# Composed weights permuted on TensorE, part of a projection and a third of the first loads moved to GpSimd, in an attention and mixture-of-experts kernel

## The chip, the cores and the metric

The kernel runs on one core of a Trainium2 chip. The metric is the time of one execution on the device in microseconds, the median of three runs. A core has five engines that run at their own pace and wait for each other by semaphores: TensorE (PE in the profile, PEld for its weight loads), VectorE (DVE), ScalarE (ACT), GpSimd (POOL) and SyncE (SP). SP does no arithmetic here; it issues DMA transfers. POOL and ACT can issue transfers too. Each engine works through its own list of instructions strictly in order.

## The reference, cut to what matters

The input is x of 4 elements x 1024 tokens x 256 channels. The kernel computes causal attention with 16 heads of 16 numbers, adds x and normalizes, then a layer of 8 experts of which each token uses 2, adds and normalizes again. The part that the change touches is the projection of x to queries and keys:

```python
q_lat = (x @ Wq_down).reshape(b, t, H, L)          # the same for k and v
q_c = jnp.einsum('bthl,ld->bhtd', q_lat, Wq_up_c)  # content half of a head
q_e = jnp.einsum('bthl,ld->bhtd', q_lat, Wq_up_e)  # half that is rotated
q = jnp.concatenate([q_c, _apply_rope(q_e, cos, sin)], axis=-1)
scores = jnp.einsum('bhqd,bhkd->bhqk', q, k) * scale
att = jax.nn.softmax(jnp.where(causal, scores, -jnp.inf), axis=-1)
y = jnp.einsum('bhqk,bhkd->bhqd', att, v)
```

## The kernel before, in words

**Composed weights.** The kernel multiplies each down matrix with its up matrix once, at its start, so that a projection is one product of x with a 256 x 256 matrix. The loop over n (0 for queries, 1 for keys, 2 for values) does this: `weffT{n}` (L206, eight products of ups and down), a copy to SBUF as `wT{n}` (L211, DVE), and four transposes by TensorE to `weff{n}` (L215). Every operand of a projection is kept as a high part (rounded to the fp32r type of TensorE, made by ACT, L190) and a low part (the rest, made by DVE or POOL, L191); the helper `split` makes both. For n = 0 and 1 the columns of `weff` must be brought from the order "pair of heads, dimension, head in the pair" to the order "dimension, head"; the kernel does this while splitting, in six pieces for each n, through a strided view.

**Projection.** `project(b, half, ...)` handles 512 tokens of element b. It splits x (`xT_h`, `xT_l`), computes four chunks of 128 rows of queries and keys (`qk_ps`: chunk 2 is the content of q, 3 the content of k, 0 and 1 the two members of the pairs to rotate for q and k), each as six products (`mm3`, L197 to L199), rotates chunks 0 and 1 (products with the table `rope`, L283 and L285, and their sum `t`, L286), and cuts each result into three bf16 parts (`store`: `lv`, with the remainder `r` between; L261, L263, L264, L265). The parts go to DRAM (`parts`, L268). Then come the values (`v_ps`, `va`). The name `lean` says which engine makes the low parts, the sums and the last bf16 part: DVE for element 0, POOL for the others. Most of the tiles have a single buffer: a second `r` or `t` can only be written when the first has been read.

**Loads of a stack.** `load_stack(unit, halves)` reads the bf16 parts of a group of four heads back from DRAM in six slots of 16 rows (c = 0 to 5) for queries (`qs`) and keys (`ks`): twelve transfers, all issued by SP (L338). The first unit (element 0, group 0) is loaded in two calls, one for each half of the tokens, because attention on the first half needs only that. Until the first half's twelve transfers have landed, there is nothing for attention to do.

**Attention.** For each unit `row_max` computes the scores (`s`, L353 and for the diagonal L370), their maxima on DVE (L374, L383), and puts the negated maxima as two extra rows into `qs` (L399). `attend` computes the scores again, transposed (`sT`, L456), the exponentials on ACT (`pT`, L462), masks the diagonal block on POOL (L474), and multiplies with the values (`y`, L437). After the attention come the experts.

**Order.** The kernel is written with a tile framework that simulates its timeline when the program is built and lets that decide the order of each engine's list. An edit in one place therefore moves instructions elsewhere. Once built, the order of every list is fixed.

Of the kernel before, what the change touches and what calls it, by code (L numbers as in the profile page):

```python
# [9 lines left out]
F32 = mybir.dt.float32  # L10
# [25 lines left out]
P = 128  # L36
# [7 lines left out]
def kernel(  # L44
# [16 lines left out]
    nc = tc.nc  # L61
    B, T, C = x_in.shape
    DH = ups_in.shape[2] // 2
    DHE = DH // 2
    H = C // DH
    E, _, FF = wg_in.shape
    NB = T // P
    CC = C // P
# [34 lines left out]
    proj = pctx.enter_context(tc.tile_pool(name="proj", bufs=1))  # L103
# [12 lines left out]
    def any_tile(name):  # L116

        turn[0] += 1
        return (mx_tile, bg_tile, mx_tile, st_tile, bg_tile, mx_tile, st_tile)[turn[0] % 7](name)
# [19 lines left out]
    def load_x(b, half):  # L139
        t = proj.tile([P, CC, QC], F32, tag="x_half", name=f"xh{b}_{half}")  # L140
        nc.sync.dma_start(
            out=t, in_=x_t[b, :, half * QC : (half + 1) * QC].rearrange("(c p) t -> p c t", p=P)
        )
        x_half[b, half] = t
# [10 lines left out]

    ident = const.tile([P, P], F32, name="ident")
    make_identity(nc, ident)
    ident_b = const.tile([P, P], BF16, name="ident_b")
    nc.vector.tensor_copy(ident_b, ident)

# [18 lines left out]
    wqk_h = proj.tile([P, CC, 4 * P], F32R, name="wqk_h")  # L179
    wqk_l = proj.tile([P, CC, 4 * P], F32R, name="wqk_l")  # L180
    wv_h = proj.tile([P, CC, C], F32R, name="wv_h")
    wv_l = proj.tile([P, CC, C], F32R, name="wv_l")
# [5 lines left out]
    def split(hi, lo, src, sub=None):  # L188

        nc.scalar.copy(hi, src)  # L190
        (sub or nc.vector).tensor_tensor(lo, src, hi.bitcast(F32), ALU.subtract)  # L191

    def mm3(ps, terms):

        n = len(terms)
        for i, (sh, sl, mh, ml) in enumerate(terms):
            nc.tensor.matmul(ps, lhsT=sh, rhs=mh, start=(i == 0), stop=False)  # L197
            nc.tensor.matmul(ps, lhsT=sh, rhs=ml, start=False, stop=False)  # L198
            nc.tensor.matmul(ps, lhsT=sl, rhs=mh, start=False, stop=(i == n - 1))  # L199


    for n in range(3):
        acc = any_tile(f"weffT{n}")
        for i in range(H // 2):
            at = i % 4 * 2 * DH
            nc.tensor.matmul(  # L206
                acc[at : at + 2 * DH, i // 4 * C : (i // 4 + 1) * C], lhsT=ups[:, n], rhs=down[n][:, i],
                start=True, stop=True,
            )
        wT = proj.tile([P, QC], F32, tag="r", name=f"wT{n}", bufs=R_BUFS)  # L210
        nc.vector.tensor_copy(wT, acc)  # L211
        acc = any_tile(f"weff{n}")
        for c in range(CC):
            for i in range(2):
                nc.tensor.transpose(  # L215
                    acc[:, (c * 2 + i) * P : (c * 2 + i + 1) * P], wT[:, i * C + c * P : i * C + (c + 1) * P], ident
                )
        if n == 2:
            split(wv_h, wv_l, acc.rearrange("p (c m) -> p c m", c=CC))
            continue  # L220
        for c in range(CC):

            src = acc[:, c * C : (c + 1) * C].rearrange("p (a d i) -> p d a i", d=DH, i=2)
            for d0, d1, at in ((0, DHE, (2 + n) * P), (DHE, DHE + 4, n * 4 * H), (DHE + 4, DH, P + n * 4 * H)):
                hi, lo = (
                    w[:, c, at : at + (d1 - d0) * H].rearrange("p (d a i) -> p d a i", a=H // 2, i=2)
                    for w in (wqk_h, wqk_l)
                )
                split(hi, lo, src[:, d0:d1])


    WAIT = -1.0
# [3 lines left out]
    def project(b, half, tile_):  # L236
        if half == 0:
            parts[b] = dram.tile([2, NQC, 3, DH, H, QC], BF16, name=f"parts{b}", tag="parts", bufs=2)
        pd = parts[b]
        n = f"{b}_{half}"  # L240
        xh = x_half.pop((b, half))
        cols = slice(half * QC, (half + 1) * QC)
        lean = nc.gpsimd if b else nc.vector
        hi = proj.tile([P, CC, QC], F32R, tag="xT_h", name=f"xT_h{n}")
        lo = proj.tile([P, CC, QC], F32R, tag="xT_l", name=f"xT_l{n}")
        for c in range(CC):
            split(hi[:, c], lo[:, c], xh[:, c], lean)
        yield 0.2
        if half + 1 < NQC or b + 1 < B:
            load_x(b + (half + 1) // NQC, (half + 1) % NQC)  # L250

        def chunk(k):
            ps = tile_(f"qk_ps{n}_{k}")
            cut = slice(k * P, (k + 1) * P)
            mm3(ps, [(wqk_h[:, c, cut], wqk_l[:, c, cut], hi[:, c], lo[:, c]) for c in range(CC)])
            return ps

        def store(k, src, sub, rows):

            lv = proj.tile([P, 3, QC], BF16, tag=f"lv{k}", name=f"lv{n}_{k}")  # L260
            nc.scalar.copy(lv[:, 0], src)  # L261
            r = proj.tile([P, QC], F32, tag="r", name=f"r{n}_{k}", bufs=R_BUFS)
            sub.tensor_tensor(r, src, lv[:, 0], ALU.subtract)  # L263
            nc.scalar.copy(lv[:, 1], r)  # L264
            lean.tensor_tensor(lv[:, 2], r, lv[:, 1], ALU.subtract)  # L265
            at = 0
            for qk, row, m in rows:
                (nc.gpsimd if b else nc.sync).dma_start(  # L268
                    out=pd[qk, half, :, row : row + m].rearrange("k d h t -> (d h) k t"),
                    in_=lv[at : at + m * H],  # L270
                )
                at += m * H

        for qk in range(2):
            store(2 + qk, chunk(2 + qk), nc.vector, [(qk, 0, DHE)])
            yield 1.3
        pair = []
        for o in range(2):
            pair.append(chunk(o))
            yield 1.3  # L280
        for o in range(2):
            t1 = proj.tile([P, QC], F32, tag="t1", name=f"t1_{n}_{o}", bufs=R_BUFS)
            nc.vector.tensor_tensor(t1, pair[o], rope[:, 2 * o, cols], ALU.mult)  # L283
            t2 = proj.tile([P, QC], F32, tag="t2", name=f"t2_{n}_{o}", bufs=R_BUFS)
            nc.vector.tensor_tensor(t2, pair[1 - o], rope[:, 2 * o + 1, cols], ALU.mult)  # L285
            lean.tensor_tensor(t1, t1, t2, ALU.add)  # L286
            store(o, t1, lean, [(qk, DHE + o * DHE // 2, DHE // 2) for qk in range(2)])
            yield 0.2
        while b >= 2 and not attended.get(b - 2):
            yield WAIT  # L290
        dst = va[b % 2][:, half * BPQ : (half + 1) * BPQ, : H * VW]
        for i in range(0, BPQ, 2):
            ps = tile_(f"v_ps{n}_{i}")
            for j in range(2):
                tok = slice((i + j) * P, (i + j + 1) * P)
                mm3(
                    ps[:, j * C : (j + 1) * C],
                    [(hi[:, c, tok], lo[:, c, tok], wv_h[:, c], wv_l[:, c]) for c in range(CC)],
                )
            for j in range(2):  # L300
                nc.scalar.copy(
                    dst[:, i + j].rearrange("p (h d) -> p h d", d=VW)[:, :, :DH],
                    ps[:, j * C : (j + 1) * C].rearrange("p (h d) -> p h d", d=DH),
                )
            yield 1.3
# [3 lines left out]
    units = [(b, (g,), tuple(range(NQC))) for b in range(B - 1) for g in range(NG)]  # L309
# [13 lines left out]
    queued = [None]  # L323

    def load_stack(unit, halves=None):
        b, gs, qcs = unit
        i = units.index(unit) % NST
        for gi, g in enumerate(gs):
            heads = slice(g * HG, (g + 1) * HG)


            for c, qk_parts in enumerate(((0, 0), (0, 1), (0, 2), (1, 0), (1, 1), (2, 0))):
                for qk, tiles in enumerate((qs, ks)):
                    wanted = halves or (range(qcs[-1] + 1) if qk else qcs)
                    f0, f1 = wanted[0], wanted[-1] + 1
                    s0 = gi if qcs == (0,) else f0
                    rows = tiles[i][:NROW].rearrange("(d c) f h t -> d c f (h t)", c=6)
                    queued[0] = nc.sync.dma_start(  # L338
                        out=rows[:, c, s0 : s0 + f1 - f0],
                        in_=parts[b][qk, f0:f1, qk_parts[qk], :, heads].rearrange("f d h t -> d f (h t)"),  # L340
                    )
# [771 lines left out]
    for i, unit in enumerate(units):  # L1113
        b, gs, qcs = unit
# [22 lines left out]
        for n, over in enumerate(attend(unit)):  # L1137
# [20 lines left out]
            at = n - HG * BPQ * (len(qcs) - 1)  # L1158
# [191 lines left out]
```

## Time and profile before

| what | value |
|---|---|
| median of 3 runs | 1103.49 us (1098.18 to 1103.93) |
| the profiled execution | 1052.3 us, span 1050.5 us |
| mean granted TensorE clock in it | 0.976 |
| busy share of the span: PE, PEld | 92%, 57% |
| DVE, ACT, POOL | 70%, 60%, 46% |
| instructions in the span | 18000 |

The span runs from the first to the last instruction of the one execution that the profiler recorded. That execution was 51 us shorter than the median of the runs. Times in the trace are microseconds from the start of the span. A row of the timeline gives start, duration, engine, line, what is written and what is read, and in brackets how long the engine had been idle and what ended the wait.

### The profile page before, as it was taken

Reading aid. Unit: us, or ns where it says so; the run is one execution under the profiler, and the core shown is the slowest. Engines: PE = TensorE matmul, PEld = TensorE weight load, DVE = VectorE, ACT = ScalarE, POOL = GpSimd, SP = SyncE. Lnnn points to the kernel's source line nnn. Section 1 sums busy time; section 2 is a strip of 40 time slices with the busy share of each in tenths; the row PEclk is TensorE's granted clock in tenths of the full one; section 3 lists DMA queues with packets and bytes.
Section 4 is the critical chain, followed back from the end, with each engine's and each line's share of the span. In section 5 each row is a group of like instructions: output and inputs, shape, how many; then the busy total and the mean of one; then the engine's idle time right before and its main releaser. Section 6 shows DMA issues by size and latency. Waiting matters only on the chain.

```text
span 1050.5 us, 18000 instructions
## 1 busy us (share of the span) xinstructions
PE 964.0 (92%) x6392; PEld 600.2 (57%) x6392; DVE 735.5 (70%) x1630; ACT 625.1 (60%) x1314; POOL 480.9 (46%) x551
## 2 busy tenths in 40 slices
PE   6689999999999999999899999999999999999960
PEld 4555433355544545554344444378888888888960
DVE  4777887888988887688547898285685546555636
ACT  3445766665666666566665676665654546565633
POOL 7176521120451813354323323754477875654535
PEclk9899999999999999999999999999999999999995
DMA  6574421221421403324222420176473765655638
GB/s 257 167 212 133 119 70 45 82 82 41 132 70 57 127 6 118 111 66 122 66 66 78 116 66 2 23 241 164 104 169 90 144 143 124 175 116 137 139 55 320
DMA packets 71362, 119.66 MB, mean 114 GB/s; under 512 B 16416, under 2 KB 43040, under 8 KB 70880
## 3 DMA queue, kind: packets, MB, share of 16 engines
q1 hardware_dynamic: 48544, 81.76, 24.7%
q0 software_dynamic: 20672, 36.41, 16.0%
q8 instruction: 52, 0.85, 0.3%
q10 hardware_dynamic: 2048, 0.27, 0.2%
q14 instruction: 46, 0.38, 0.1%
HBM read 82.52 MB, written 35.60 MB: 112 GB/s over the span
## 4 chain that ended last, share of the span: by engine, by line
PE 73%; DVE 8%; DMA 6%; ACT 5%; SPq 3%; issue 3%; POOL 2%; ACTq 0%; DVEq 0%; POOLq 0%
PE y L437 13%; PE s L353 11%; PE sT L456 11%; PE gp L198 3%; SPq L338 3%; PE gp L199 3%; PE gp L197 3%; PE eo L197 3%; PE eo L198 3%; PE eo L199 3%; PE po L623 2%; ACT pT L462 2%; PE s L370 2%; PE lp L199 2%; PE lp L198 2%
## 5 line engine op out<-in xcount | busy, mean ns | idle before, releaser
L462 ACT ACTIVATE pT<-sT 128x512 f32<-128x512 f32 (+1 forms) x608 | 326.6, 576 | 160.9 <-PE sT L456 132.4
L374 DVE TENSOR_REDUCE mx<-s 128x1 f32<-128x384 f32 (+3 forms) x352 | 215.8, 632 | 41.6 <-PE s L370 40.2
L353 PE MATMUL s<-ks,qs 96*128 96x512 bf16 (+3 forms) x768 | 211.7, 330 | 15.1 <-DMA ks<-parts 7.7
L456 PE MATMUL sT<-qs,ks 98*128 98x512 bf16 (+3 forms) x768 | 212.9, 329 | 8.8 <-ACT pT L462 6.7
L474 POOL TENSOR_SCALAR_AFFINE_SELECT pT<-pT 128x512 f32<-128x512 f32 x120 | 75.7, 637 | 270.7 <-ACT pT L462 263.8
L383 DVE TENSOR_REDUCE mx<-s 128x1 f32<-128x512 f32 x256 | 171.2, 681 | 30.9 <-PE s L353 29.8
L437 PE MATMUL y<-pT,va 128*32 128x512 f32 (+3 forms) x1536 | 171.3, 501 | 1.0 <-POOL pT L474 0.6
L1028 POOL DMA_INDIRECT results<-eo,ents x64 | 105.3, 1646 | 79.1 <-ACT eo L1027 65.1
L353 PEld LDWEIGHTS <-qs 96*128 96x128 bf16 x768 | 70.8, 99 | 110.8 <-issue 83.2
L456 PEld LDWEIGHTS <-ks 98*128 98x128 bf16 x768 | 68.9, 98 | 95.0 <-issue 61.9
L370 PE MATMUL s<-mask,ident_b 128*128 128x128 bf16 (+2 forms) x352 | 86.6, 247 | 0.0
L1011 DVE TENSOR_TENSOR relu<-relu,lp 128x512 f32<-128x512 f32 x64 | 43.7, 683 | 60.2 <-ACT relu L1010 37.3
L191 DVE TENSOR_TENSOR wl<-w,wh 128x512 fp32r<-128x512 f32 x108 | 69.6, 684 | 22.3 <-ACT wh L190 20.7
L197 PE MATMUL eo<-wh,hh 128*128 128x256 f32 x280 | 80.9, 291 | 2.7 <-ACT eo L1027 2.2
L198 PE MATMUL eo<-wl,hh 128*128 128x256 f32 x280 | 78.7, 283 | 0.0
L954 POOL DMA_INDIRECT xg<-x_rows,ents x64 | 65.9, 1030 | 26.6 <-issue 15.8
L1010 ACT ACTIVATE relu<-gp 128x512 f32<-128x512 f32 (+1 forms) x76 | 42.7, 564 | 58.9 <-PE gp L199 58.4
L199 PE MATMUL eo<-wh,hl 128*128 128x256 f32 x280 | 77.3, 282 | 0.0
L846 POOL DMA_INDIRECT pairs<-ent,so_i x64 | 64.6, 1009 | 25.3 <-issue 17.5
L191 DVE TENSOR_TENSOR hl<-relu,hh 128x512 fp32r<-128x512 f32 (+1 forms) x76 | 48.4, 645 | 28.5 <-ACT hh L190 27.8
L437 PEld LDWEIGHTS y<-pT,va 128*32 128x32 f32 x1536 | 32.1, 108 | 62.3 <-issue 46.8
L190 ACT CAST wh<-w 128x512 fp32r<-128x512 f32 x108 | 60.7, 619 | 11.2 <-PE gp L198 6.9
(212 smaller groups left out, 1846.1 us busy)
## 6 DMA issues: line engine op xcount, KB each, us to landing
ks<-parts SPq DMA_DIRECT2D x90, 128.0 KB, 3.1
w<-in_wg_dram SPq DMA_DIRECT2D x18, 512.0 KB, 4.5
w<-in_wp_dram SPq DMA_DIRECT2D x18, 512.0 KB, 5.6
w<-in_wo_dram SPq DMA_DIRECT2D x18, 512.0 KB, 4.1
qs<-parts SPq DMA_DIRECT2D x66, 128.0 KB, 2.7
parts<-lv POOLq DMA_DIRECT2D x12, 384.0 KB, 3.0
parts<-lv POOLq DMA_DIRECT2D x24, 192.0 KB, 3.2
xh<-in_x_t_dram SPq DMA_DIRECT2D x8, 512.0 KB
```

Source lines behind the costliest of these rows:

```text
L191: (sub or nc.vector).tensor_tensor(lo, src, hi.bitcast(F32), ALU.subtract)
L197: nc.tensor.matmul(ps, lhsT=sh, rhs=mh, start=(i == 0), stop=False)
L198: nc.tensor.matmul(ps, lhsT=sh, rhs=ml, start=False, stop=False)
L199: nc.tensor.matmul(ps, lhsT=sl, rhs=mh, start=False, stop=(i == n - 1))
L353: nc.tensor.matmul(ps, lhsT=q(h, half)[:NROW, t * P : (t + 1) * P], rhs=k(h, kc)[:NROW, :w], start=first, stop=last,)
L370: nc.tensor.matmul(each[:, :, w - P :], lhsT=ident_b, rhs=mask.unsqueeze(1).to_broadcast([P, m, P]), start=False, stop=True,)
L374: nc.vector.tensor_reduce(mx_of[:, half, h0 : h0 + m, t], each, AX.X, ALU.max)
L383: nc.vector.tensor_reduce(mx_of[:, kc, h, t : t + 1], ps, AX.X, ALU.max)
L437: nc.tensor.matmul(acc[g, qc][SLOT * h : SLOT * (h + 1), lo:], lhsT=va[b % 2][:, kb, at : at + SLOT], rhs=pT[:, h, lo:], start=(kb == 0), ...
L456: nc.tensor.matmul(st[:, h % m * w : (h % m + 1) * w], lhsT=k(h, kb // BPQ)[: NROW + 2, kb % BPQ * P : (kb % BPQ + 1) * P], rhs=q(h, qc)[: ...
L462: nc.scalar.activation(pT[:, h + 1 - m : h + 1, lo:], st[:, : m * w].rearrange("p (h t) -> p h t", t=w), AF.Exp, scale=scale,)
L1028: ins = nc.gpsimd.indirect_dma_start(out=results[:, :], out_offset=bass.IndirectOffsetOnAxis(ap=k.ent[:, j, 1:2], axis=0), in_=eo, in_offs ...
```

## The change

It has three parts.

1. A matrix `by_row` is made once by DVE from the identity: the identity with its columns permuted. For n = 0 and 1 the four transposes are replaced by four ordinary fp32 products with `by_row` as the moving operand, so that `weff` comes out of TensorE already in the order "dimension, head" (written to PSUM in runs of eight). The split of each n then needs two pieces of 256 columns instead of six.
2. `lean` becomes POOL for the second half of element 0 too. Five kinds of instruction move from DVE to POOL there: both `xT_l`, four `lv` (last part), two sums `t`, and the two remainders `r` of the rotated chunks.
3. In both calls of `load_stack` for the first unit, the loads of `ks` in the slots c = 2 to 5 are issued by POOL instead of SP: four of twelve in each call.

```diff
+    by_row = proj.tile([P, P], F32, name="by_row")
+    nc.vector.tensor_copy(
+        by_row.rearrange("p (d a i) -> p d a i", a=4, i=2), ident.rearrange("p (a d i) -> p d a i", a=4, i=2)
+    )
...
         acc = any_tile(f"weff{n}")
+        if n == 2:
+            for c in range(CC):
+                for i in range(2):
+                    nc.tensor.transpose(
+                        acc[:, (c * 2 + i) * P : (c * 2 + i + 1) * P], wT[:, i * C + c * P : i * C + (c + 1) * P],
+                        ident,
+                    )
+            split(wv_h, wv_l, acc.rearrange("p (c m) -> p c m", c=CC))
+            continue
+
+        rows = acc.rearrange("p (c d i m) -> p c d i m", c=CC, d=DH, i=2)
         for c in range(CC):
             for i in range(2):
-                nc.tensor.transpose(
-                    acc[:, (c * 2 + i) * P : (c * 2 + i + 1) * P], wT[:, i * C + c * P : i * C + (c + 1) * P], ident
+                nc.tensor.matmul(
+                    rows[:, c, :, i], lhsT=wT[:, i * C + c * P : i * C + (c + 1) * P], rhs=by_row,
+                    start=(c == i == 0), stop=(c == i == 1),
                 )
-        if n == 2:
-            split(wv_h, wv_l, acc.rearrange("p (c m) -> p c m", c=CC))
-            continue
-        for c in range(CC):
-
-            src = acc[:, c * C : (c + 1) * C].rearrange("p (a d i) -> p d a i", d=DH, i=2)
-            for d0, d1, at in ((0, DHE, (2 + n) * P), (DHE, DHE + 4, n * 4 * H), (DHE + 4, DH, P + n * 4 * H)):
-                hi, lo = (
-                    w[:, c, at : at + (d1 - d0) * H].rearrange("p (d a i) -> p d a i", a=H // 2, i=2)
-                    for w in (wqk_h, wqk_l)
-                )
-                split(hi, lo, src[:, d0:d1])
+        acc = acc.rearrange("p (c m) -> p c m", c=CC)
+        split(*(w[:, :, (2 + n) * P : (3 + n) * P] for w in (wqk_h, wqk_l)), acc[:, :, :P])
+        split(
+            *(w[:, :, : 2 * P].rearrange("p c (k m) -> p c k m", k=2)[:, :, :, n * 4 * H : (n + 1) * 4 * H]
+              for w in (wqk_h, wqk_l)),
+            acc[:, :, P:].rearrange("p c (k m) -> p c k m", k=2),
+        )
...
-        lean = nc.gpsimd if b else nc.vector
+        lean = nc.gpsimd if b or half else nc.vector
...
-                    queued[0] = nc.sync.dma_start(
+
+                    queue = nc.gpsimd if units.index(unit) == 0 and qk and c > 1 else nc.sync
+                    queued[0] = queue.dma_start(
                         out=rows[:, c, s0 : s0 + f1 - f0],
                         in_=parts[b][qk, f0:f1, qk_parts[qk], :, heads].rearrange("f d h t -> d f (h t)"),
                     )
```

As built, the changed program has these orders around the edits. On PE, `weffT` and `weff` of n = 0 and 1 and then `weffT` of n = 2 all stand ahead of the first projection product; before, three projection products stood ahead of `weffT` of n = 2. On POOL, the first four loads of `ks` stand behind `xT_l` (2), `lv` of chunk 2 and the sum `t` of chunk 0 of the second half, and ahead of `xT_l` (2) of element 1, `lv` of chunk 3 and `r` of chunk 0; the second four stand behind `lv` of chunk 2 of element 1. On DVE, the last product of the rotation of the second half stands ahead of the first row maximum. On PE, the 24 products `v_ps` of the first half of element 1 stand behind the first scores of the second half of element 0; before, they stood ahead of them. From the last group of the third element on, PE's list is the same as before, except that the routing of the last element stands up to 66 rows later among the first experts.

## The prediction

> **What bounds the kernel now.** I read the page first, for the busy shares and the 40 slices.
>
> ```profile
> span 1050.5 us, 18000 instructions
> PE 964.0 (92%) x6392; PEld 600.2 (57%) x6392; DVE 735.5 (70%) x1630; ACT 625.1 (60%) x1314; POOL 480.9 (46%) x551
> PE   6689999999999999999899999999999999999960
> ```
>
> PE is busy 92% of the span, and its slices are at 9 nearly everywhere. The holes are in the first three slices (26 us each) and in the last. All three edits act in the first three. Second view: the busy time of each engine by stage (after the stretch: PE, PEld, DVE, ACT, POOL with counts, granted clock, DMA share, GB/s).
>
> ```profile
> 27.00:40.00 13.00, 11.29 (x59) 8.99 (x57) 9.15 (x15) 6.93 (x16) 2.52 (x2) 1.00 0.50 146
> 40.00:47.00 7.00, 0.32 (x4) 0.35 (x5) 4.71 (x7) 1.94 (x4) 0.00 (x0) 0.77 0.48 142
> 47.00:57.00 10.00, 8.04 (x39) 4.90 (x36) 8.88 (x16) 2.77 (x5) 5.41 (x5) 0.82 0.85 255
> 57.00:64.00 7.00, 5.09 (x27) 4.62 (x27) 1.35 (x3) 3.78 (x10) 5.77 (x6) 0.76 0.40 113
> 64.00:80.00 16.00, 15.88 (x101) 8.38 (x100) 13.93 (x23) 9.01 (x17) 11.30 (x14) 1.00 0.86 259
> 80.00:100.00 20.00, 18.04 (x99) 11.58 (x97) 13.96 (x26) 9.55 (x20) 13.83 (x15) 0.91 0.44 120
> ```
>
> Up to 64 us PE waits; from 64 us it is full, and DVE nearly so. So a start-up that ends earlier is worth only what PE's idle time shrinks by. Third view, the chain that ended last in order of time (start, duration, what):
>
> ```profile
> 33.56 0.60 DVE lv L265
> 34.18 2.82 DMA parts<-lv
> 37.09 0.55 SPq L338
> ...
> 44.01 2.32 DMA ks<-parts
> 46.33 0.35 issue
> 46.68 0.58 PE s L353 x4
> ...
> 48.57 5.62 DMA parts<-lv
> 54.21 0.54 SPq L338
> ...
> 61.17 2.20 DMA qs<-parts
> 63.37 0.25 issue
> 63.62 0.39 PE s L353
> ```
>
> It shows two gates of one form. The last bf16 part is made, its store lands, SP issues loads one by one 0.63 us apart (37.09 to 44.01 for the last of twelve), the last load lands, scores begin: at 46.68 us for the first half of the tokens, at 63.62 us for the second. PE is idle 7.1 us ahead of the first gate and 1.6 us directly ahead of the second.
>
> **Part 1, the weights.** Removed: twelve ACT casts (four of 0.267 us, eight of 0.212: 2.8 us) and twelve DVE subtractions (4 x 0.289 + 8 x 0.224 = 2.9 us). Added: four of each with 256 columns; the nearest rows are ACT's copy of 128x256 at L616 (0.37 us) and DVE's addition of 128x256 at L626 (0.42 us), together 3.2 us. So 2.5 us of work goes. It was on PE's path only as far as PE waited for it, and as built PE puts `weffT` of n = 2 ahead of the first projection product. In the trace that one starts at 15.69 us, released by the landing of its matrix. The gain ends there. The products with `by_row` are not in the trace. Lower bound: the transposes that they replace, four in 0.66 us. Upper bound: the fp32 products at L623, recorded twice for each product and 0.215 us apart, 8 x 0.215 = 1.7 us; that row is the nearest, and I take 1.6, so 0.5 to 0.9 us more for each n. Then `weff` of n = 0 ends at 9.93 + 1.6 = 11.5, `weffT` of n = 1 at 13.4, its copy at 14.2, `weff` of n = 1 at 15.8, `weffT` of n = 2 at 16.9. Chunk 0 is the third of four at 6 x 0.228 us each: done at 21.0 instead of 20.4, and chunk 1, behind `weff` of n = 2, at 22.8 instead of 22.05. This part costs 0.6 us on the path. The copy `by_row` (0.35 us, by the cast of the identity) is hidden: DVE is idle until 8.49 us. If it weren't, it would cost its 0.35.
>
> **Part 2, first half.** DVE's last `lv` of the first half ends at 34.16. Between 20.43 and there it runs 19 instructions 0.60 us apart; as built, four leave that stretch (two `xT_l` go to POOL, two rotation products of the second half stand behind it): 2.4 us. Less the 0.6 of part 1. There is a rule against it: the Trainium skill, "SBUF — State Buffer", section "Who interferes with whom", says that a DVE instruction with both inputs in SBUF and a GpSimd instruction that reads SBUF exclude each other for a whole instruction. The trace has one meeting:
>
> ```profile
> 35.64 2.52 POOL L191 TENSOR_TENSOR xT_l<-xh,xT_h 128x512 fp32r<-128x512 f32 x2 [16.05 <-ACT xT_h L190]
> 37.69 1.02 DVE L265 TENSOR_TENSOR lv<-r,lv 128x512 bf16<-128x512 f32 x1 [1.74 <-ACT lv L264]
> ```
>
> The DVE instruction took 1.02 instead of 0.69 us and ended after POOL's pair. By this row the price is 0.33 us; by the rule up to one POOL instruction, 1.26 us, since `xT_l` now lies beside the remainders and parts of the first half. I take 0.3, keep 1.3. The last `lv` ends at 34.16 - 2.4 + 0.6 + 0.3 = 32.7, and its store, 2.8 us as before, lands at 35.5.
>
> **Part 3, first gate.** SP now has eight loads: the last is issued 7 x 0.63 us after 35.5, at 39.9, and lands 2.3 us later, 42.2. POOL's four wait for the same stores. POOL comes to them after `lv` of chunk 2 (its `r` at 33.3, cast to 34.3, 1.16 us) and the sum (1.28 us), at 36.8. An issue on POOL costs 0.63 to 1.03 us, median 0.67, in the row of its stores; four take 3.0, and the last, started at 39.2, lands 3.0 us later (median of that row, 2.8 to 4.3), 42.2. Scores begin at about 42.5 instead of 46.7. Here another sentence speaks against the change: the Trainium skill, "DMA: Bandwidth & Descriptors", section "Issuing engines are not separate DMA queues", says that issuing from several engines saves only the sequencer's time, usually small beside the transfer. By the rule the move is worth next to nothing; by the chain of waits the issue itself is the path, 4 x 0.63 = 2.5 us. I follow the trace.
>
> **Part 2, second half: what queues behind POOL.** POOL does its list at 1.26 (`xT_l`), 1.16 (`lv`, `r`) and 1.28 us (`t`), where DVE has 0.60. After the four issues (39.8) come `xT_l` of element 1 (42.3), `lv` of chunk 3 (43.5), `r` of chunk 0 (44.7). DVE's last rotation product waits for that `r`, and the row maxima stand behind it: they start at 45.4 instead of 47.7, and the eleven, 0.605 us each and without the four other instructions that lay among them, end at 52.1 instead of 56.8. On POOL follow, with a cast of 0.65 us by ACT between, `lv` (46.5), the sum (47.8), `r` (49.6), `lv` of chunk 1 (51.5). Its stores stood at 48.57 before; they are 2.9 us later. There they took 5.6 us to land, behind 0.5 MB of x; now x is issued about 9 us sooner, and I take 3.5, so 55.0 instead of 54.2. Eight issues and the landing, 4.4 + 2.2, give 61.6, scores at 61.8 instead of 63.6. POOL's second four start at 55.0 too and land by 60.2. If POOL's list were 1.8 us longer, this gain would be gone.
>
> **The account on PE.** At 63.6 us the trace has the 24 `v_ps` products (57.44 to 62.0) done; as built they now come after the second gate: 24 x 0.12 = 2.9 us still owed. Ahead of the gate stand instead five `sT` at 0.22: 1.1 us. So -1.8 + 2.9 - 1.1 = 0.0. The four microseconds at the first gate do not reach the end, because PE finds little to do between the gates. What can come back is idle PE behind 64 us: 2.1 us in 64 to 100, nearly all waits for row maxima. DVE and ACT (five exponentials, 2.7 us) are ahead there, so I take 2.0 us.
>
> **Order farther on.** PE's list differs from before by up to some 80 places until the third element. Idle PE from 64 to 500 us sums to 13.1 us. I take zero, and 4 us either way: a third of it.
>
> **Sum.** -2.0 us on 1052.3, which is the profiled execution. The median shown is 1103.5, 51 us longer; what changes is waiting for DVE, POOL and queues, so I carry the microseconds over unscaled: 1101.5.
>
> **The rivals.**
>
> 1. *POOL becomes the gate of the second half (slower).* For: POOL needs 12 us for what took DVE half, in series with ACT's casts, and the loads stand in the same list. With the lock at its upper end (+1), issues at 1.03 us, and the store landing in 5.6 us as before, the second gate comes at 64.8: 1.2 later than before, and with the owed 1.8 us on PE the loss is 3.0 us, 1106.5. It decides from a gate at 61.8 on, a microsecond for each microsecond. With an order that loses 4 as well: 1110.5. Against: at 51.5 POOL has only its own list to follow, and the queue is emptier.
> 2. *The earlier row maxima carry through (faster).* For: DVE is 87% busy from 64 to 80 us and PE waits for it; maxima that end 4.7 us sooner let the pipeline start full. If the whole 4.2 us of the first gate stays, 1099.3; with an order that gains 4, 1095. Against: PE, at 15.88 of 16 us, has no room to use it.
> 3. *Nothing arrives*: the projection is bound by the third matrix and the second gate is where it was: within 2 us of 1103.5. That the edits do not what they say is excluded by the orders as built.
>
> **How the numbers follow.** A measurement of this kernel tells some 0.5% (5.5 us) from no change. Main case with the third rival: 0.55, mostly inside that. Rival 2: 0.27, rival 1: 0.18. Past 5.5 us lie most of rival 2 with a good order, and a tenth of the main case: 0.33 faster. Rival 1 with a bad order and a part of the main case: 0.2 slower. 0.47 within. The range of 8 in 10 reaches from rival 2 with a good order and the runs' own spread (1091) to rival 1 with a bad order (1110); the main case alone would be 1097 to 1106.
>
> **What would show it.** Right: `weffT` of n = 2 still starting near 15.8 and chunk 0 not before 20.5; first scores near 42.5, first maxima near 45.4, the last `lv` of POOL near 51.5, second gate near 62, the 24 `v_ps` behind it; PE busy from there. Wrong: a second gate past 64; DVE parts of over 1 us beside POOL's `xT_l`; more than 15 us of idle PE between the gate and 500 us, or under 9.

## The result, and the profile after

The changed kernel takes 1113.11 us (median of 6 runs, 1108.80 to 1117.03), the kernel before 1100.77 us beside it (6 runs, 1098.18 to 1103.93): a ratio of 1.0095, interval 1.0070 to 1.0119. It is slower by 12 us, where 1101.5 was forecast.

One thing has to be known to read the numbers. The runs of one group share a chip, and there are two kinds of chip for this kernel: before takes 1101 to 1107 us in some groups and 1054 to 1055 us in others. The profile of before shown above (1052.3 us) belongs to the second kind, the result above to the first. Ratios compare within a group only. "Long chip" and "short chip" stand for the two kinds below; the profile of before on a long chip is that of the run e0_control. A trace is one execution, and traces of two groups come from two chips: between them a few microseconds can be the chip or the execution.

The page of the changed kernel (long chip):

```profile
span 1112.1 us, 17995 instructions
PE 992.9 (89%) x6400; PEld 609.9 (55%) x6400; DVE 736.6 (66%) x1613; ACT 624.5 (56%) x1306; POOL 493.6 (44%) x569
PE   6689999999988999998999998699999699999970
```

The three slices of the start are as before; the slices with 6 are at about 700 and 860 us, and before has such slices on a long chip too. The start-up by stage (PE, PEld, DVE, ACT, POOL, granted clock, DMA share, GB/s):

```profile
40.00:47.00 7.00, 3.30 (x8) 2.12 (x8) 0.69 (x1) 2.00 (x5) 6.07 (x8) 0.70 0.51 160
47.00:57.00 10.00, 7.01 (x34) 4.08 (x34) 7.71 (x14) 3.42 (x7) 5.64 (x5) 0.84 0.50 138
57.00:64.00 7.00, 5.81 (x17) 3.26 (x17) 2.08 (x3) 3.45 (x7) 5.17 (x8) 0.79 0.62 172
64.00:80.00 16.00, 13.63 (x92) 7.32 (x92) 9.56 (x15) 7.55 (x18) 11.26 (x13) 0.89 0.81 243
```

From 64 to 80 us PE is no longer full: 13.63 us instead of 15.88. POOL, idle from 40 to 47 us before, is now busy for 6.07 of 7. The chain that ended last:

```profile
10.17 2.08 PE weff L231 x8
...
14.93 2.07 PE weff L231 x8
17.01 1.87 PE weffT L211 x16
...
29.33 1.70 DVE r L275
...
31.74 0.98 DVE lv L277
...
35.39 0.70 DVE lv L277
...
36.74 3.43 DMA parts<-lv
...
40.82 0.78 POOL ks L352
...
42.60 0.48 POOL ks L352
43.10 2.51 POOL xT_l L196 x2
...
54.86 1.17 POOL lv L277
56.04 2.83 DMA parts<-lv
58.92 0.53 SPq L352
...
63.28 2.94 DMA qs<-parts
66.23 0.14 issue
66.36 0.38 PE s L367
```

Between the two gates the chain now runs through POOL, from its loads of `ks` to its last `lv`. The second gate opens at 66.36 us. In e0_control, on the same kind of chip, it opens at 65.31, and in the profile of before shown above at 63.62:

```profile
65.07 0.25 issue
65.31 0.39 PE s L353
```

A gate also moves from one execution to the next. The five traces with the lists of the changed kernel up to 200 us have it at 63.59, 64.22, 66.17, 66.36 and 67.04 us, and the four with those of before at 63.62, 63.69, 64.77 and 65.31. A difference of a microsecond between two single traces therefore shows little.

Where do 12 us go? The order of the lists differs, so equal times are not equal work. I therefore added up TensorE's products, each counted with the median start-to-start interval of its form over the traces (the whole kernel is then about 758 us of work, 760 with part 1), and read from each trace when a given amount was done:

```
work  | short chip:                         | long chip:
done  | before  changed  v_early  dm_act    | before  changed  v_early  dm_act  v_late
 80   |  134.4    140.4    140.7    137.8   |  136.1    139.8    146.6   139.5   140.1
200   |  312.6    321.0    316.8    318.4   |  314.0    320.3    322.8   320.0   318.5
220   |  343.4    362.4    349.8    355.0   |  344.9    361.8    355.5   356.8   349.4
340   |  523.7    536.9    529.5    528.8   |  534.6    544.8    539.7   534.3   531.8
440   |  688.1    698.5    691.8    694.4   |  720.1    728.1    722.6   711.2   716.5
540   |  792.4    810.4    802.2    802.4   |  827.5    836.9    831.3   818.3   821.6
760   | 1015.5   1038.9   1028.4   1030.9   | 1071.1   1076.8   1067.1  1053.8  1059.5
```

(v_early, dm_act and v_late are experiments 5, 7 and 6.) The sum is rough. Most of the products `y` are recorded 7 ns after the one before them, so they count for almost nothing, although a group of eight lasts a microsecond or more; and the products with `by_row` count 2.5 us more as progress at the start. The long columns come from three groups: there the traces of the changed kernel and of before end only 5.7 us apart, where the runs side by side differ by 12. A mark that needs no sum is the last `y`, with which the attention ends. In the order of the columns it starts at 682, 699, 692 and 693 us on the short chip, and at 715, 728, 723, 710 and 711 on the long one.

On either chip the changed kernel is 4 to 6 us behind at 80 us of work and 6 to 8 at 200. Then it falls back by 10.6 us, on both alike, within 20 us of work: the step from 200 to 220. This place is not in the start-up. Experiment 7, which has the same lists up to 200 us, falls back by 5.9 and 5.8 us there. So 4.7 and 4.8 us of the step are one hole that experiment 7 removes; of the rest I cannot say how much is time and how much the rough sum. The hole in the timeline of the changed kernel:

```profile
327.33 0.27 DVE L740 TENSOR_REDUCE sk_nm<-sk_tp 8x1 f32<-8x128 f32 x1
327.64 3.65 DVE L745 TENSOR_SCALAR sk_dm<-ident,sk_nm 8x8 f32<-8x8 f32 x1
327.66 1.17 POOL L275 TENSOR_TENSOR r<-t,lv 128x512 f32<-128x512 f32 x1
328.78 2.47 POOL L196 TENSOR_TENSOR xT_l<-xh,xT_h 128x512 fp32r<-128x512 f32 x2
331.20 0.67 DVE L388 TENSOR_REDUCE mx<-s 128x1 f32<-128x512 f32 x1
331.93 0.38 PE L367 MATMUL s<-ks,qs 96*128 96x512 bf16 x1 [3.02 <-DVE mx L388]
```

`sk_dm` is an 8x8 product of the router (three for each element). It usually takes 0.22 us. Here it is placed at the moment at which POOL begins three operations on SBUF without a gap, and it takes 3.65 us, until they end. The row maximum behind it on DVE is late by that, PE waits 3.02 us for it, and then its granted clock falls:

```profile
328.00:332.00 4.00, 0.98 (x8) 0.49 (x6) 4.00 (x3) 2.38 (x7) 3.25 (x3) 1.00 0.18 48
332.00:337.00 5.00, 4.78 (x22) 1.78 (x22) 3.42 (x12) 2.06 (x6) 1.76 (x2) 0.60 0.36 105
337.00:343.00 6.00, 4.94 (x21) 2.52 (x22) 1.78 (x6) 2.22 (x6) 2.58 (x4) 0.50 0.36 88
```

From the drop on, PE runs at half clock for some 10 us (4.0 of the 5 us of the second stretch, by its mean of 0.60, and the 6 of the third). The same hole is in the short chip's trace of the changed kernel (3.65 us at 328.32). No part of the change touches the router, or anything at 330 us; the built order brought the two instructions together.

### The profile page after: what moved, and what is told of

Read it like the earlier page. It is cut to its first block, busy times and chain, and to the rows that moved or that the text cites. A ratio compares the mean times of both kernels' runs of the same rounds, so it can differ in the third digit from the quotient of the medians.

```text
span 1112.1 us, 17995 instructions
## 1 busy us (share of the span) xinstructions
PE 992.9 (89%) x6400; PEld 609.9 (55%) x6400; DVE 736.6 (66%) x1613; ACT 624.5 (56%) x1306; POOL 493.6 (44%) x569
## 4 chain that ended last, share of the span: by engine, by line
PE 73%; DVE 8%; ACT 5%; DMA 5%; issue 3%; POOL 2%; another core or an unknown queue 1%; SPq 1%; ACTq 0%; DVEq 0%; POOLq 0%
PE y L451 14%; PE sT L470 11%; PE s L367 10%; PE gp L203 3%; ACT pT L476 3%; PE gp L204 3%; PE gp L202 3%; PE eo L202 3%; PE eo L203 3%; PE eo L204 3%; PE po L637 2%; PE lp L203 2%; PE lp L204 2%; PE lp L202 2%; PE s L384 2%
## 5 line engine op out<-in xcount | busy, mean ns | idle before, releaser
L470 PE MATMUL sT<-qs,ks 98*128 98x512 bf16 (+3 forms) x768 | 215.2, 333 | 26.0 <-ACT pT L476 18.2
L451 PE MATMUL y<-pT,va 128*32 128x512 f32 (+3 forms) x1536 | 178.7, 508 | 1.4 <-ACT yT L456 0.9
L202 PE MATMUL gp<-xh,wh 128*128 128x512 f32 (+1 forms) x176 | 64.3, 372 | 3.7 <-ACT xh L195 1.5
```

Source lines behind the costliest of these rows:

```text
L451: nc.tensor.matmul(acc[g, qc][SLOT * h : SLOT * (h + 1), lo:], lhsT=va[b % 2][:, kb, at : at + SLOT], rhs=pT[:, h, lo:], start=(kb == 0), ...
L470: nc.tensor.matmul(st[:, h % m * w : (h % m + 1) * w], lhsT=k(h, kb // BPQ)[: NROW + 2, kb % BPQ * P : (kb % BPQ + 1) * P], rhs=q(h, qc)[: ...
```

## The experiments

The expectations name four theories. A: GpSimd's longer list makes the second gate late, and that is most of the loss. B: the new order of the lists farther on is most of it. C: part 1 alone costs, since the projections start later. D: the 24 value products that now stand behind the second gate are the loss.

"Moved" below means: instructions of TensorE's list (9054) outside the longest sequence that both lists share in the same order. Against before, the changed kernel has 2006 moved.

**Group 1 (long chip, before 1105.81 us): one part at a time.**

1. e0_control: before itself.

> The kernel before, unchanged, run for its trace: the profile shown before was an execution of 1052 us, while the runs of that kernel take about 1100 us. All theories expect 1.000 +- 0.003 against before. The trace should put the second gate (first scores of the second half) at about 63.6 us again; if the 48 us between 1052 and 1100 lie behind the start-up (idle TensorE in the attention and the experts), the trace shows where, and only this trace may be set beside the changed kernel's.

Measured 1107.02 us, 1.0000 (0.9983 to 1.0017). The group can tell 0.2%.

2. e1_weights: part 1 alone.

```diff
-                nc.tensor.transpose(
+                nc.tensor.matmul(
+                    rows[:, c, :, i], lhsT=wT[:, i * C + c * P : i * C + (c + 1) * P], rhs=by_row,
```

> Part 1 alone (weights leave TensorE in the order of use; all else as before). Theory A (the GpSimd list makes the second gate late and that is most of the loss): 0 to +2 us, since the products with by_row cost 1.0 and 1.4 us at the start and the gates move by that. Theory B (the new order of the lists farther on is most of the loss, whatever part causes it): anything from -5 to +8 us, with the two gates moved by less than 2 us. Theory C (part 1 alone costs: weffT of the third matrix and all projections start 2.2 us later): +2 to +4 us, both gates 2 us later.

Measured 1101.03 us, 0.9954 (0.9935 to 0.9974): faster, although both gates are later than in e0_control (49.88 and 66.93 us instead of 48.25 and 65.31; in group 5 again, 49.18 and 66.79 instead of 48.33 and 64.77).

3. e2_lean: part 2 alone.

```diff
-        lean = nc.gpsimd if b else nc.vector
+        lean = nc.gpsimd if b or half else nc.vector
```

> Part 2 alone (low parts, sums and last bf16 parts of the second half of element 0 on GpSimd). Theory A: +4 to +8 us, second gate at 65 us or later, because GpSimd needs about twice DVE's time for the same list. Theory B: gates as theory A says or earlier, but the loss lies in idle TensorE behind 100 us. Theory C: within 2 us of before.

Measured 1113.05 us, 1.0065 (1.0045 to 1.0085). The first scores come at 47.83 us, those of the second half only at 70.20 instead of 65.31. That isn't GpSimd's doing: SP issues the last of the twelve loads at 63.02 us (62.87 in e0_control), but PE's list puts the value products and some `y` ahead of those scores. The built order also has a collision of its own, in another place:

```profile
92.80 1.30 POOL L268 DMA_DIRECT2D parts<-lv  x2 [0.30 <-POOL lv L265]
93.36 4.49 DVE L389 TENSOR_TENSOR mx<-mx 128x16 f32<-128x16 f32 x1
94.11 1.28 POOL L286 TENSOR_TENSOR t<-t,t 128x512 f32<-128x512 f32 x1
95.34 2.47 POOL L191 TENSOR_TENSOR xT_l<-xh,xT_h 128x512 fp32r<-128x512 f32 x2
97.91 0.28 PE L392 MATMUL mxT<-ident,mx 128*16 128x128 f32 x1 [3.39 <-DVE mx L389]
```

4. e3_loads: part 3 alone.

```diff
-                    queued[0] = nc.sync.dma_start(
+                    queue = nc.gpsimd if units.index(unit) == 0 and qk and c > 1 else nc.sync
+                    queued[0] = queue.dma_start(
```

> Part 3 alone (four of the twelve first loads of each half issued by GpSimd). Theory A: -1 to -4 us, both gates about 2.5 us earlier, because eight issues take 5.0 us where twelve take 7.5. Theory B: the same gates, and a total that does not follow them (-5 to +8 us). Theory C: -1 to -3 us.

Measured 1118.84 us, 1.0111 (1.0064 to 1.0159). Both gates are earlier than in e0_control (47.24 and 61.81 us), and it is the slowest of the four. It has the collision of `sk_dm` too (3.63 us at 322.8).

What follows: the gates and the total go opposite ways in two of three, and in the third the loads are not late. A start-up gate cannot be the main cause.

**Group 2 (long chip, before 1101.66 us): the order by itself.**

5. e9_v_early: the changed kernel, with the order of before around the second gate asked for. `project(1, 0)` is laid out whole ahead of the attention, and the scores of the second half are ordered behind its last value product.

```diff
+    for _ in early:
+        pass
+    last_of["values"] = last_of["mm3"]
...
+                if unit == units[0] and half == 1:
+                    tc.add_manual_dep(
+                        ins.ins, last_of["values"].ins.name,
+                        mybir.DependencyInfo(mybir.DependencyClass.NoSync, mybir.DependencyReason.SCHED_ONLY),
```

> The changed kernel with all three of its parts, and one rule more for the builder's order on TensorE: the second half's first score stands behind the 24 value products (v_ps) of element 1's first half, which are laid out ahead of the attention. Nothing else is asked for; as built, the lists then lie 442 places (of 9054 on TensorE) from those of the kernel before, where the changed kernel lies 2006 places away. Theory A (GpSimd's list makes the second gate late, and that is the loss): GpSimd's list for the first element is the same, so the gate stays at 65 to 67 us and the ratio at 1.008 to 1.012. Theory B (the order of the lists farther on is the loss, and the parts matter by the order that they cause): the ratio falls to 0.992 to 1.002, with no hole of 3 us on TensorE near 330 us. Theory D, new (the 24 value products that lay in the hole between the gates and now come behind it are the loss by themselves): 2.9 us of products at full clock, about 5 as they ran in the hole: ratio 1.004 to 1.006.

Measured 1099.42 us, 0.9996 (0.9976 to 1.0017). All three parts are in, and the loss against before is gone, although the scores of the second half come later than anywhere else, by the order asked for:

```profile
73.37 0.83 PE L369 MATMUL s<-ks,qs 96*128 96x512 bf16 x6
```

The changed kernel itself did not run in this group; its 1.0095 is from the group of the result. `sk_dm` takes no more than its usual time near 320 us; the longest wait of the router is 2.56 us (`sk_dg`), which before has as well (2.58 us at 303.8).

6. e8_v_late: before, with only the 24 products held behind the first score of the second half.

```diff
+            if held:
+                behind_gate(ins, gate["scores"])
```

> The kernel before, with the same 24 value products held behind the first score of the second half, by a rule of order alone. As built, 105 of 9054 places on TensorE differ from before and nothing of the loads, of GpSimd's work or of the weights. Theory D (the products are the loss): 1.003 to 1.007, and the whole of it must be there by 100 us. Theory B: the order farther on is nearly that of before, so 0.998 to 1.003. Theory A: 1.000, since no gate moves.

Measured 1098.97 us, 0.9984 (0.9961 to 1.0007). It is 4.0 us behind the trace of before (another chip) at 80 us of work and 2.8 ahead at 340, and in the runs side by side it is level: a start-up that is late by 4 us need not arrive at the end. The products are not the cause.

7. e7_after_dm_act: the changed kernel with `sk_dm` on ACT.

```diff
-            nc.vector.tensor_scalar(dm, ident[:E, :E], nm, None, ALU.mult)
+            nc.scalar.activation(dm, ident[:E, :E], AF.Copy, scale=nm)
```

> The changed kernel with one small operation of the router moved from VectorE to ScalarE: the 8x8 product sk_dm, which in the profile of the changed kernel took 3.65 us instead of 0.22 at 327.6 us while GpSimd ran three operations on SBUF in a row, and behind which TensorE waited 3.0 us and then ran at half clock for 10.2 us. The lists move 897 places on TensorE, all behind 200 us. Theory B, with collisions of VectorE and GpSimd as its mechanism: that hole goes, worth 3 us of idle and up to 5 of clock, ratio 1.002 to 1.006, unless another operation falls into the same place, which the profile would show. Theories A and D: 1.008 to 1.012, since nothing ahead of 200 us changes.

Measured 1093.99 us, 0.9954 (0.9928 to 0.9980): more than expected. POOL still runs `r` and both `xT_l` in a row (327.24 to 330.88), but now beside row maxima, which read PSUM and take 0.67 us as ever. The same stages:

```profile
328.00:332.00 4.00, 3.49 (x24) 1.48 (x24) 3.96 (x9) 3.02 (x9) 4.00 (x5) 1.00 0.12 31
332.00:337.00 5.00, 4.10 (x20) 1.02 (x20) 1.93 (x7) 2.77 (x7) 3.10 (x5) 0.66 0.65 182
337.00:343.00 6.00, 5.04 (x32) 1.85 (x30) 1.47 (x5) 4.50 (x12) 1.16 (x2) 1.00 0.48 144
```

The clock falls here too, beside a wait of 1.09 us at 332.90, but for 3.4 us only (0.66 over 5 us). So the hole costs 1.9 us more of waiting and, by my estimate, half of the other 6.6 us at half clock: 5 us together, close to the 4.7 of the table.

By the table it has won 10.5 us at 340 of work, and 6.4 more at 440. The second part is another place of the order, near 690 us. In e0_control the chain there is POOL's run of sixteen scatters of the router's pairs, with the `rstd` of a normalization behind them on the same engine, and the attention behind that:

```profile
670.76 1.02 POOL pairs L846
...
689.80 0.96 POOL pairs L846
...
691.13 1.05 POOL rstd L551
...
692.54 1.06 DVE x L553 x3
693.61 0.61 ACT pT L462
```

PE's longest wait there is 6.5 us in e0_control and 6.7 in the changed kernel; in e7 none is over 1.7.

8. e10_before_dm_act: before with the same edit, so that nothing of the start-up changes.

> The kernel before with the same move of sk_dm from VectorE to ScalarE, as the control of the run before it: 409 places on TensorE move, none of them ahead of about 200 us, and the work is the same but for twelve operations of 0.2 us on another engine. In before the operation that waited (2.58 us at 303.8) is sk_dg, not sk_dm, and TensorE lost 1.6 us by it. Theories A and D: 1.000. Theory B: anything from 0.994 to 1.006, which would itself show what an order is worth.

Measured 1096.18 us, 0.9953 (0.9933 to 0.9973), though its own collision is still there (`sk_dg`, 3.12 us at 303). So 409 moved places, with twelve operations of 0.2 us taken off DVE, are worth half a per cent; the two were not separated. e7 is then no clean price of the collision: some of its gain can be of this kind. Something else is clean. e7 and e10 ran side by side and differ by the change alone: with `sk_dm` on ACT in both kernels the three parts cost nothing that the runs can tell on a long chip (0.9954 and 0.9953).

**Group 3 (short chip, before 1054.29 us).** These four ran on the other kind of chip, and none compares with groups 1 and 2.

9. e11_after_dm_psum: the changed kernel with the result of `sk_dm` in PSUM.

```diff
-            dm = sinkp.tile([E, E], F32, tag="sk_dm", name=f"sk_dm{b}_{it}")
+            dm = tp[:E, 3 * P : 3 * P + E]
```

> The changed kernel with the result of the 8x8 product sk_dm left in a free corner of the router's PSUM tile instead of SBUF. It stays on VectorE, and neither it nor the operation that reads it (sk_dg) then has two operands in SBUF beside GpSimd. As built, 713 places on TensorE move, none ahead of about 200 us. Theory B with the collision as its mechanism: as by the move of sk_dm to ScalarE, 0.995 to 1.003, and no VectorE instruction of the router over 1.3 us between 290 and 340 us. If the gain of that move was only a lucky order: 1.006 to 1.012. Theory A: 1.008 to 1.012.

Measured 1068.38 us, 1.0131 (1.0094 to 1.0169). The router's waits are gone (the longest between 290 and 340 us is a `mx` of 1.53).

10. e12_v_early_dm_psum: experiment 5 with the edit of 9.

> All three parts of the change, the rule that puts the 24 value products ahead of the second half's scores, and the PSUM result of sk_dm; 342 places on TensorE from the run with the rule alone. Theory B: the rule alone gave 0.9996 and still had a collision of sk_dg (2.56 us at 316.7); without it 0.990 to 0.998. Theory A: 1.008 to 1.012, because the second gate is late (73.4 us with the rule).

Measured 1066.67 us, 1.0104 (1.0071 to 1.0137).

11. e13_weights_dm_psum: part 1 alone with the edit of 9.

> A candidate to beat both kernels: part 1 alone (the weights, 0.9954) with the PSUM result of sk_dm, whose kernel has a collision of sk_dg of 2.56 us at 307.0 too; 333 places on TensorE from part 1 alone. Theory B: 0.988 to 0.996. If collisions are no cost by themselves: 0.993 to 0.998, as before.

Measured 1065.18 us, 1.0095 (1.0069 to 1.0121). What theory B expected failed in all three: on this kind of chip these orders lose 1% against before. The numbers lie at theory A's ranges (e12 inside, e11 just above), but e13 has no part 2 and loses too. By the same sums e13 is ahead of before at 440 us of work and 10 us behind at 700: its loss is in the experts. Some 6 us of it arise in one place, where TensorE's records have the same order in both: at 842 us PE waits 1.14 us for a gathered tile and 1.87 for ACT, and then needs about 0.21 us for each product `eo` instead of 0.12. Why ACT was late was not traced.

12. e4_no_weights: parts 2 and 3.

> Parts 2 and 3 without part 1 (the weights as before). If the parts add up, this is the changed kernel less the gain of part 1, or part 2 (1.0065) and part 3 (1.0111) together: 1.014 to 1.018. Theory B: as built, its lists lie 116 places on TensorE from those of the changed kernel and 1935 from those of before, so it belongs to the same order, with the same collision of sk_dm (about 3.6 us near 325 us), and is as slow as part 3 alone and the changed kernel are: 1.009 to 1.012.

Measured 1070.76 us, 1.0157 (1.0133 to 1.0181), without the changed kernel beside it not to be judged. Hence the next group.

**Group 4 (short chip, before 1055.23 us): the changed kernel and its remedies side by side.**

> The changed kernel itself, as the reference of this group. On a chip where before takes about 1100 us: 1.007 to 1.012 by its own runs. On one where before takes about 1054 us: by the four runs there 1.010 to 1.018.

13. e14_changed_again, the changed kernel: 1074.12 us, 1.0171 (1.0146 to 1.0197).

> The changed kernel with the rule that puts the 24 value products ahead of the second half's scores. Theory B (order of the lists): less than the changed kernel beside it by 0.8 to 1.2 points on either kind of chip. If the order matters only through waits that exist where before takes 1100 us: there as before (0.998 to 1.002), and on the other kind level with the changed kernel beside it. Theory A: level with the changed kernel on both.

14. e15_v_early_again, as 5: 1067.83 us, 1.0134 (1.0098 to 1.0170). It takes away 0.37 points of 1.71 (6.3 us by the medians), with intervals that overlap: a part of the loss at most.

> The changed kernel with sk_dm on ScalarE. Theory B with the collision: less than the changed kernel beside it, by 0.5 to 0.8 points for the hole at 330 us alone (3 us of idle and up to 5 of clock) on either kind of chip; the first run had 1.4 points, of which 0.9 came at about 690 us, where TensorE waited in the changed kernel behind GpSimd's run of sixteen scatters. On a chip without that wait only the 0.5 to 0.8 is left.

15. e16_dm_act_again, as 7: 1067.23 us, 1.0107 (1.0078 to 1.0137). It takes away 0.64 points, 6.9 us, with intervals that do not overlap: what was expected of the hole alone. The stretch of the hole, first in before, then in the changed kernel, then in this one:

```profile
320.00:360.00 40.00, 38.46 (x276) 19.05 (x273) 34.87 (x86) 25.82 (x53) 17.67 (x21) 1.00 0.21 65
```

```profile
320.00:360.00 40.00, 33.64 (x210) 15.46 (x202) 25.71 (x75) 24.00 (x55) 17.22 (x20) 0.87 0.29 83
```

```profile
320.00:360.00 40.00, 36.38 (x233) 16.59 (x232) 26.81 (x77) 27.01 (x63) 18.13 (x22) 0.96 0.31 93
```

> Parts 2 and 3 without part 1, 116 places on TensorE from the changed kernel. Theory B: within 0.25 points of the changed kernel beside it. If parts add up: 0.46 points more than it.

16. e17_no_weights_again, as 12: 1070.34 us, 1.0151 (1.0117 to 1.0185), beside 1.0171 for the changed kernel: level with it within the intervals, and not above it. It has the same collision (3.64 us at 325.0), and its list has 116 moved from that of the changed kernel, 1935 from that of before. The parts do not add up here. Its trace also speaks against theory A on a short chip: the second gate opens at 63.62 us, as in the profile of before, and the kernel still loses 1.5%.

**Group 5 (long chip, before 1105.88 us).** What these two do on a short chip stays open; on a long one they repeat.

> The kernel before with sk_dm on ScalarE: the start-up and the first 200 us are before's, 409 places on TensorE move behind them. It gave 0.9953 where before took 1102 us. Theory B (order alone moves the time): on a chip where before takes 1055 us it loses although nothing of the change is in it, 1.004 to 1.010. If the parts of the change are what costs there: 0.995 to 1.000.

17. e18_before_dm_act_again, as 8: 1099.53 us, 0.9932 (0.9908 to 0.9956).

> Part 1 alone, which gave 0.9954 where before took 1106 us. Theory B: on a chip where before takes 1055 us it loses too, 1.004 to 1.011 (1.0095 was measured there for part 1 with the PSUM result of sk_dm). If part 1 by itself is a gain of work: 0.994 to 0.999 on both kinds of chip.

18. e19_weights_again, as 2: 1100.61 us, 0.9957 (0.9934 to 0.9979). On a long chip e1, e7 and e10 beat both kernels; on a short one nothing that I ran beat before.

## Why the prediction was wrong, point by point

- *Order farther on, "zero, and 4 us either way".* This is the step that failed. Idle time of PE in before cannot bound it: a new order makes holes that before does not have. The one at 330 us is worth about 5 us, and by my estimate 3 of them are clock, for which the sum had no term. The prediction's own sign showed: PE was idle for 19.6 us between the gate and 500 us (16.9 in e0_control), over the 15 named. Shown by the runs: with another order the same three parts are level on a long chip (0.9996), and so they are with `sk_dm` on ACT in both kernels, so there the order is the whole of the net loss. On a short chip the moved `sk_dm` took away 0.64 points of 1.71 and the rule of order 0.37, which is not clear of noise; the rule with the PSUM form of `sk_dm` still lost 1.04% there. The cause of that rest stays open.
- *Part 1, 0.6 us on the path.* The mechanism held, the size did not: four products with `by_row` took 2.08 us for each n, not 1.6, `weffT` of n = 2 ended at 18.9, not 16.9, and DVE began on the first half's results at 23.27 instead of 20.43. The size is not fixed: in e16, with the same lists up to 200 us, the second four took 1.16 us and `weffT` ended at 17.1. The profile of before had shown as much: its four transposes took 1.08 us for n = 0 and 0.66 for n = 1. I allowed for that in the transposes, and not in the products, whose 1.6 came from rows at 216 us and later. The whole part is no loss on a long chip; where its gain comes from (order or less work) was not separated.
- *Price of the lock, 0.3 us.* I followed the one meeting in the trace (0.33) against the Trainium skill, "SBUF — State Buffer", section "Who interferes with whom". The rule was nearer. DVE's `r` at 29.33 took 1.70 us instead of 0.69 beside `xT_l` (29.17 to 32.17), and an `lv` 0.98: 1.3 us, the upper bound that I kept. The last `lv` of the first half ended at 36.1 instead of 32.7, and its store landed at 40.2, 4.7 us after the predicted 35.5.
- *First gate, 42.5 us.* It came at 47.16. The saving of issues was there: POOL's four took 2.26 us (I had 3.0). What they waited for was late.
- *Second gate, 61.8 us.* The queueing behind POOL's loads was right, and passed the delay on: POOL's last `lv` ended at 56.0 instead of 51.5, and the gate came at 66.36, past the 64 that I had named as the sign of being wrong.
- *The account on PE.* Rival 1's formula holds roughly for the start-up. On the long chip a gate later by 1.05 us plus the 1.8 us owed gives 2.9, and the table has 3.7 at 80 us of work. (On the short chip the gate is 3.4 us later and the lag 6.0; but e16, with the same lists and on the same chip, has 0.6 and 3.4.) That it must arrive at the end was wrong: e8 had the same lag and lost it again.
- *Regained 2.0 us of idle PE.* Not seen: PE is busy 13.63 of 16 us from 64 to 80, and its idle time from 64 to 100 grew from 2.1 to 5.4 us (3.4 in e0_control).
- *Rival 1 (slower, 1106.5, with a bad order 1110.5)* had the right sign and the right start-up, but 3 of the 12 us; its "bad order" was the larger part and was sized at 4.

What stays open: on a short chip some 17 of the 23 us between the two traces are there when the attention ends, and the hole is about 5 of them. The other 7 come in the experts, where PE's list is that of before apart from the routing of the last element; they were not traced to one place.

## What to carry to other kernels

Where a builder chooses the order of the lists, an edit's price is its own path plus the price of a new order, and the second can be the larger: give it a range from runs of orders that change little or no work (here up to half a per cent on one kind of chip), and ask for the order by a rule before judging an edit. Look in the trace for short instructions that took many times their usual duration; they are cheap to move to another engine and can stand ahead of everything that matters. A gate that opens earlier proves nothing about the end.

## What the runs showed of the hardware that was not expected

- A DVE instruction that meets POOL on SBUF can wait not for one POOL instruction but for a whole row of them: 3.65 us for 1.17 + 2.47, and 4.49 for the rest of a DMA issue, 1.28 and 2.47, however small it is (8x8). It need not: in e7 `sk_dg` took 0.20 us at 329.54, in the middle of such a row. The section named above speaks of the whole of one instruction.
- A hole of 3.02 us on PE was followed by 10 us at half the granted clock. The Trainium skill, "TensorE: Matmul & The Clock Gate", section "HAM oscillation — how this bites in real kernels", warns of idle gaps above about 3.4 us; here a shorter one stood ahead of the drop, and in e7 a wait of 1.09 us ahead of a drop of 3.4 us. The length of one gap did not tell.
- The same kernel takes 1054 or 1105 us by the chip. The two traces of before keep a constant lag of 1.3 us until 369 us and then part mostly around POOL's scatters of pairs: 3.3 us at the first four, 14 at the sixteen near 660 us and about 20 at those near 800. On a long chip other engines stand still beside them, ACT for example at 685.06 for 5.03 us, with no releaser that the profile names. The reason was not found.
